# Moving mixer work between slots: frequencies, first convolution, ranks, and the second experts' preparation

## The chip, the cores and the metric

The kernel runs on one core of one Trainium2 chip. A core has five engines with queues of their own, each of which takes its instructions strictly in order: TensorE (PE in the profile; PEld are its weight loads), VectorE (DVE), ScalarE (ACT), GpSimd (POOL) and SyncE (SP), which here only issues DMAs. They wait for each other by semaphores. The metric is the device time of one execution in microseconds (us). Before the change, three runs gave 2046.63, 2048.35 and 2057.33 us; the median is 2048.35 us.

## The reference, cut to what matters

The whole is two macaron layers over 8 sequences of 256 tokens, 128 features each: a cell FFN, attention, the cell FFN again, then experts, a mixer, and the same experts a second time. The change lies in the last three:

```python
x = x + 0.5 * _L1_ffn_ref(_layernorm(x), gate_w, w1, w2, w3)      # first experts
x = x + _L1_attn_ref(_layernorm(x), ...)                          # the mixer
x = x + 0.5 * _L1_ffn_ref(_layernorm(x), gate_w, w1, w2, w3)      # second experts
```

The experts choose the two best of 8 gates for each token, scale the token by them, and apply two matmuls with a `silu` and a third. The mixer has a forward and a backward branch of this kind, and a Fourier branch:

```python
x = silu(_causal_dwconv(x, conv_w, conv_b))
x_dbl = einsum('bdl,ed->bel', x, xproj_w)
dt, Bm, Cm = (x_dbl[:, :r], x_dbl[:, r:r + n], x_dbl[:, r + n:])
delta = softplus(einsum('brl,dr->bdl', dt, dtproj_w) + dt_bias)
dA = exp(einsum('bdl,dn->lbdn', delta, -exp(A_log)))
dBu = einsum('bdl,bnl,bdl->lbdn', delta, Bm, x)
# scan over l: h = dA * h + dBu;  y = sum over n of h * Cm, + Dp * x, all times silu(z)
...
xc = silu(conv(fftn(x)) + fft_conv_b); x_out = ifftn(xc)
v = abs(x_out * max(silu(z))); out_f = (v - mean(v)) / sqrt(var(v) + 1e-05)
y = out + out_b[:, :, ::-1] + out_f;  return einsum('bdl,od->blo', y, out_proj_w)
```

## The kernel before

The tokens are cut into 4 chunks of 512 (two sequences each). All work of experts and mixer is placed by hand in numbered **slots** by `experts_and_mixer` (L799): `at(slot, f, ...)` files a function under a slot, and a loop at its end (L1582 to L1595) emits the slots one after the other, on TensorE, VectorE, ScalarE and GpSimd in just that order. Slot 32 c + s is called "slot s of chunk c" here; chunks are numbered 0 to 3. In each slot the loop emits a fixed core and then what was filed:

```python
scan(i)
feed(i + 1)
for f in before.get(i, ()):
    f()
if i % 2:
    sums(i - 3)
for f in after.get(i, ()):
    f()
...
spread(i + 2, *range(m, m + more))
```

The core handles one of 128 units (32 of each chunk). `spread` (L1179) puts delta times input (`pU`) and the delta (`p`) of the unit two slots ahead on all 128 partitions with 32-row matmuls, and ScalarE makes the decays `dA` of `p` (L1181). `feed` (L1188) multiplies `pU` by B on VectorE. `scan` (L1199) is the recurrence on VectorE; GpSimd multiplies its result by C (`hc`, L1201). `sums` (L1218) adds this up on TensorE every second slot. `pU` has two buffers, `h` two, `hc` four, and all other matmuls of the mixer share three PSUM banks (`bank`, L846). The number of decays made per slot, `more`, drops to 0 for two slots at each of two places of a chunk and catches up in the next five.

Between these stand, for the chunk that comes next (`ch`, filed from `o = (ch - 1) * UNITS`): `normalize` (L1027; layer norm, parts 0 and 1 are statistics, 2 and 3 the scaling on ScalarE), `features` (L1038; four transposes and a copy into `xT`), `convolve` (L1056; four matmuls each), `gate`, the `silu`s, `ranks` (L1087; two matmuls of 96 columns and the copy to `low`), `steps` (L1108; dt projection, ScalarE makes `ab` and `dl` of it), `softplus` (L1126) and `delta` (L1131; `dl` plus `ab` on VectorE, times `u` on GpSimd, then two DMAs on SP that make `du` with swapped halves). `steps`, `softplus` and `delta` run twice for each chunk, for two groups of channels `t`. For the Fourier branch, `frequencies` (L1230) is made of the next chunk's normalized tokens, `pairs` (L1241) on GpSimd, `mix` (L1251; ten matmul records and a copy) eight times, `mirror` (L1268) on GpSimd, then, from slot 27 into the next chunk, `halves` (`sp`, L1281), `over_channels` (L1297), `folds` (`t`, L1308), `over_tokens` (L1314), `squares` and the statistics, and at last `join` (L1396; GpSimd), `output` (L1402; sixteen matmul records) and `add` (L1418; GpSimd, the residual). In the last chunk the Fourier work is packed into the chunk itself. B and C rows are copied by DMA (`rows`, L1099) in slots 24, 26, 32 and 34.

The **second experts** (`class Experts`, L936) work on chunk c after its mixer residual is added. `prepare` (L1431) files `statistics` (VectorE and GpSimd) in slot k, `scale` (four activations that write `exn` on ScalarE) and `transpose` (four matmuls, copy to `exT`) in k + 1, `logits` in k + 2 and `gates` (VectorE) in k + 3. The buffer of `exn` is that of the mixer's `ab`, the one of `exT` that of `sz`. The matmuls of the experts themselves (`step`) follow from slot 129 on, one token tile to a slot, with the last two preparations among them: this is the tail.

Of the kernel before, what the change touches and what calls it, by code (L numbers as in the profile page):

```python
# [798 lines left out]
def experts_and_mixer(nc, tc, ident, nhalf, x, cols, ins, w, given, store):  # L799
# [19 lines left out]
    with ExitStack() as ctx:  # L819
# [23 lines left out]
        def at(slot, f, *a, last=False):  # L843
            (after if last else before).setdefault(slot, []).append(lambda: f(*a))
# [576 lines left out]
        def u_of(ch, t):  # L1421
            return lambda: (gots[ch]["u", t], None)

        def sz_of(ch):
            return lambda: (gots[ch]["sz"], None)

        def sc_of(ch, co):
            return lambda: (gots[ch]["sc"][:, co], fft_b[:, co : co + 1])

        first, second = Experts(given=given), Experts(store=store)  # L1430
        def prepare(experts, c, k, *room):  # L1431

            at(k, experts.statistics, c)
            at(k + 1, experts.scale, c, *room)
            at(k + 1, experts.transpose, c, last=True)
            at(k + 2, experts.logits, c, last=True)
            at(k + 3, experts.gates, c, last=True)
# [26 lines left out]
            return rooms["xn"][:, c % 2], rooms["xT"][:, c % 2]  # L1464

        end = NCH * UNITS
        prepare(second, 0, end - 9, room)
        prepare(second, 1, end - 4, room)
        for n in range(NCH * NT + 2):
            at(end + 1 + n, second.step, n)  # L1470
        prepare(second, 2, end + 3, room)
# [22 lines left out]
        for ch in range(NCH):  # L1494

            o = (ch - 1) * UNITS
            if ch == 0:
                at(-8, ranks, ch, 1)
                at(-8, largest, ch)
                at(-7, steps, ch, 0, 0)  # L1500
                at(-6, steps, ch, 0, 1)
                at(-6, exponentials)
                at(-6, softplus, ch)
            else:
                for part, k in enumerate((-23, -22, -1, -1)):
                    if ch == 1 and part < 2:
                        k = -6
                    at(o + (0 if ch == 1 and part > 1 else k), normalize, ch, part)
                at(o, features, ch, last=True)
                at(o + 2, convolve, ch, 1, 0)  # L1510
                at(o + 6, convolve, ch, 1, 1)
                at(o + 8, convolve, ch, 0, 0)
                at(o + 10, convolve, ch, 0, 1)
                at(o + 12, silu, u_of(ch, 1), u_of(ch, 0))
                at(o + 12, gate, ch, 0)
                at(o + 12, gate, ch, 1)
                at(o + 12, silu, sz_of(ch))
                at(o + 12, exponentials)
                at(o + 15, ranks, ch, 0)
                at(o + 16, ranks, ch, 1)  # L1520
                at(o + 17, steps, ch, 0, 0)
                at(o + 17, steps, ch, 0, 1)
                at(o + 18, softplus, ch)
                at(o + 22, largest, ch)
                at(o + 28, frequencies, ch, 0, last=True)
                at(o + 28, frequencies, ch, 1, last=True)
            at(o + (26 if ch == 0 else 19), delta, ch, 0, 0)
            at(o + (26 if ch == 0 else 19), delta, ch, 0, 1)
            v = o + (6 if ch == 0 else 0)
            at(v + 30, steps, ch, 1, 0)  # L1530
            at(v + 30, steps, ch, 1, 1)
            at(v + 31, softplus, ch)
            at(v + 32, delta, ch, 1, 0)
            at(v + 33, delta, ch, 1, 1)
            for r in range(2):
                at(o + 24 + 8 * r, rows, ch, r, 0)
                at(o + 26 + 8 * r, rows, ch, r, 1)
            o += UNITS
            for t in range(2):
                at(o + 16 * t + 3, skip, ch, t, 0)  # L1540
                at(o + 16 * t + 4, skip, ch, t, 1)
                at(o + 16 * t + 18, weigh, ch, t)
            if ch == 0:
                at(o - 2, frequencies, ch, 0)
                at(o - 1, frequencies, ch, 1, last=True)

            final = ch + 1 == NCH
            for k in (1, 2):
                at(o + (k - 1 if final else 2 * k + 4), pairs, ch, k)
            mixes = (6, 8, 10, 11, 13, 14, 16, 17) if final else (11, 13, 18, 20, 22, 23, 24, 25)  # L1550
            for k, v in enumerate(mixes):
                at(o + v, mix, ch, k // 2, k % 2, last=True)
                if k % 2:
                    at(o + v + 1 + (v == 13 and not final), mirror, ch, k // 2)
            k = o + (19 if final else 27)
            bursts.add(k)
            if not final:
                bursts.add(o + 12)
            at(k, silu, *(sc_of(ch, co) for co in range(4)))
            at(k, exponentials)  # L1560
            at(k + 2, halves, ch, 0)
            at(k + 3, halves, ch, 1)
            late = (8, 9, 10, 11) if final else (9, 10, 12, 14)
            for i in range(4):
                at(k + 4 + i, over_channels, ch, i // 2, i % 2, last=True)
                at(k + (6, 7, 8, 9)[i] + (not final), folds, ch, i // 2, i % 2)
                at(k + late[i], over_tokens, ch, i // 2, i % 2, last=True)
                at(k + late[i] + 1, squares, ch, i // 2, i % 2)
            rest = (13, 14, 15, 16, 17, 18, 18) if final else (16, 17, 18, 20, 22, 31, 32)
            at(k + rest[0], magnitude, ch)  # L1570
            at(k + rest[1], moments, ch, 0)
            at(k + rest[2], moments, ch, 1)
            at(k + rest[3], whiten, ch, 0)
            at(k + rest[3], whiten, ch, 1)
            at(k + rest[4], join, ch)
            at(k + rest[5], output, ch)
            at(k + rest[6], add, ch)
# [55 lines left out]
def tile_kernel(ctx: ExitStack, tc: tile.TileContext, ins, out):  # L1633
# [98 lines left out]
    with tc.tile_pool(name="w_mixer", bufs=1) as wp:  # L1732
        names = ("inT", "inK", "xproj", "dtT", "sel", "FT", "ysel", "outT", "G")
        w = load(wp, names, "s_")
        w["conv"] = wp.tile([P, 2, 5, 2 * DI], F32, name="w_conv")
        w["D"] = wp.tile([P, 4, P], F32, name="w_D")
        experts_and_mixer(nc, tc, ident, nhalf, x, cols, ins, w | w_moe, given, store)
# [124 lines left out]
```

## Time and profile before

| stretch | us |
|---|---|
| median of the runs | 2048.35 |
| the profiled execution | 2048.99 |
| its span, first to last instruction | 2047.2 |
| before slot 0 of the mixer (FFNs, attention, set-up) | 1425.1 |
| slots 0 to 127 of the mixer | 547.1 |
| tail: second experts | 75.0 |

| what | mean us of one | times, whole kernel |
|---|---|---|
| `scan` on VectorE, L1199 | 2.28 | 128 |
| `feed` on VectorE, L1188 | 1.22 | 128 |
| `hc` on GpSimd, L1201 | 2.36 | 128 |
| one `dA` activation on ScalarE, L1181 | 0.68 | 256 |

The span is counted from the first instruction to the last; the execution's own time is 1.8 us longer. Starts of slots are the starts of their scans. The stage table that follows in the prediction gives, for each stretch of the span, the time that each engine was busy and how many instructions it ran; then the granted TensorE clock as a share of full speed, the share of DMA time and the traffic. Rows in order of time give start, length, engine, line, operation, written and read tiles, and in brackets how long the engine sat idle before, and what ended that. Records of TensorE overlap, since matmuls are pipelined.

### The profile page before, as it was taken

What the parts mean: (1) busy time and instruction counts of PE and PEld (TensorE: products, weight loads), DVE (VectorE), ACT (ScalarE), POOL (GpSimd) and SP (SyncE); (2) the same over time, 40 slices, a digit from 0 to 9 for tenths busy, and PEclk for the clock granted to TensorE, in tenths of its full rate; (3) what the DMA queues carried; (4) which work ended last, traced back from release to release, by engine and by line L of the source; (5) the groups of instructions that cost most, each with busy time, mean ns of one, the idle gap of its engine ahead of it and who ended that gap; (6) DMA issues with size and microseconds to landing.
All of it is one profiled execution on the core that took longest, in us unless ns stands there. A gap on an engine that the chain in (4) does not pass through costs nothing. (4 is left out here: it accounts for less than half of the span.)

```text
span 2047.2 us, 45119 instructions
## 1 busy us (share of the span) xinstructions
PE 1936.4 (95%) x17792; PEld 1131.6 (55%) x17792; DVE 1559.3 (76%) x2669; ACT 1143.3 (56%) x2197; POOL 809.2 (40%) x919
## 2 busy tenths in 40 slices
PE   6999999997999999899999999889999999989888
PEld 4666666654565666566666665554343344344345
DVE  5777777776777777677777778555988897898874
ACT  3777777753333232377777776445546654654444
POOL 3000000115666665300000001444777878788763
PEclk9999999998999999999999999789999999999899
DMA  4000000000000000000000000202000000000000
GB/s 146 3 2 3 3 3 3 3 2 1 2 2 2 2 2 2 2 3 3 3 3 3 3 3 3 109 22 73 11 21 21 1 22 21 11 21 11 1 1 21
DMA packets 21239, 29.23 MB, mean 14 GB/s; under 512 B 12506, under 2 KB 13914, under 8 KB 20260
## 3 DMA queue, kind: packets, MB, share of 16 engines
q1 hardware_dynamic: 20740, 26.15, 4.3%
q8 instruction: 141, 2.31, 0.5%
q14 instruction: 70, 0.57, 0.1%
q10 hardware_dynamic: 288, 0.20, 0.0%
HBM read 16.10 MB, written 1.05 MB: 8 GB/s over the span
## 5 line engine op out<-in xcount | busy, mean ns | idle before, releaser
L344 DVE TENSOR_REDUCE negmax<-sc 128x2 f32<-128x512 f32 x768 | 490.7, 681 | 158.6 <-PE sc L338 158.2
L349 ACT ACTIVATE ex<-sc 128x512 f32<-128x512 f32 x768 | 420.9, 609 | 199.4 <-PE sc L338 199.1
L338 PE MATMUL sc<-qk,qk 32*128 32x256 f32 x6144 | 471.4, 405 | 10.7 <-DVE negmax L344 9.9
L338 PEld LDWEIGHTS sc<-qk,qk 32*128 32x128 f32 x6144 | 295.8, 186 | 147.4 <-ACT ex L349 100.8
L1201 POOL TENSOR_TENSOR hc<-h,C 128x1024 f32<-128x1024 f32 x128 | 301.4, 2356 | 112.2 <-DVE h L1199 108.0
L1199 DVE TENSOR_TENSOR_SCAN h<-dA,pU 128x1024 f32<-128x1024 f32 x128 | 292.1, 2282 | 12.8 <-DVE pU L1188 0.5
L299 ACT ACTIVATE qk<-pp,w_bqk,head_rows 128x256 f32<-128x256 f32 x384 | 197.3, 572 | 73.5 <-PE pp L419 34.7
L85 POOL TENSOR_SCALAR ln_ve<-ln_mv 128x2 f32<-128x2 f32 (+1 forms) x56 | 13.3, 237 | 550.5 <-DVE ln_mv L83 545.1
L1181 ACT ACTIVATE dA<-p,cols 128x512 f32<-128x512 f32 x256 | 162.2, 684 | 110.0 <-PE p L1179 108.0
L377 PE MATMUL pc<-ex,va 128*32 128x256 f32 x3072 | 206.0, 386 | 0.2 <-DVE y L442 0.2
L1188 DVE TENSOR_TENSOR pU<-pU,B 128x1024 f32<-128x1024 f32 x128 | 155.6, 1216 | 61.1 <-PE p L1179 52.1
L621 ACT ACTIVATE ex<-sc 128x512 f32<-128x512 f32 x128 | 66.1, 603 | 204.8 <-PE sc L606 204.8
L1179 PE MATMUL pU<-du,s_sel 32*128 32x512 f32 x512 | 147.5, 650 | 20.6 <-DVE h L1199 14.3
L1179 PE MATMUL p<-dl,s_sel 32*128 32x512 f32 x512 | 156.3, 643 | 4.3 <-ACT dA L1181 4.2
L606 PE MATMUL sc<-rot,rot 32*128 32x256 f32 x2048 | 135.2, 388 | 1.3 <-POOL rot L589 1.3
L377 PEld LDWEIGHTS pc<-ex,va 128*32 128x32 f32 x3072 | 80.7, 109 | 96.6 <-issue 61.8
L198 POOL TENSOR_SCALAR w_bqk<-pb,head_rows 128x2 f32<-128x2 f32 x12 | 3.5, 313 | 299.2 <-DVE pb L195 292.2
L606 PEld LDWEIGHTS sc<-rot,rot 32*128 32x128 f32 x2048 | 97.9, 184 | 36.2 <-issue 23.1
L624 POOL TENSOR_TENSOR both<-ex 128x512 f32<-128x512 f32 x64 | 80.0, 1272 | 71.2 <-ACT ex L621 71.2
L616 DVE TENSOR_REDUCE anegmax<-sc 128x2 f32<-128x512 f32 x128 | 79.4, 684 | 24.5 <-PE sc L606 24.5
L1179 PEld LDWEIGHTS pU<-du,s_sel 32*128 32x128 f32 x512 | 40.7, 186 | 91.2 <-issue 69.0
L988 DVE TENSOR_TENSOR hid<-ph,gate 128x1024 f32<-128x1024 f32 x32 | 39.1, 1221 | 66.1 <-PE ph L983 64.5
(292 smaller groups left out, 3173.1 us busy)
## 6 DMA issues: line engine op xcount, KB each, us to landing
qk<-turned SPq DMA_DIRECT2D x768, 1.0 KB
s_fft<-s_fft SPq DMA_DIRECT2D x5, 1024.0 KB
du<-ab SPq DMA_DIRECT2D x16, 256.0 KB
B<-low SPq DMA_DIRECT2D x64, 32.0 KB
C<-low SPq DMA_DIRECT2D x64, 32.0 KB
x<-x SPq DMA_DIRECT2D x4, 256.0 KB
s_inK<-s_inK SPq DMA_DIRECT2D x1, 1024.0 KB
out<-x SPq DMA_DIRECT2D x4, 256.0 KB
```

Of the source, the lines that this page charges most:

```text
L299: nc.scalar.activation(t[:, g, :], pp, AF.Identity, scale=w["mask"][:, g : g + 1], bias=w["bqk"][:, c, i, g : g + 1],)
L338: nc.tensor.matmul(sc[:, t, :], lhs[:, t * P : (t + 1) * P], rhs, start=True, stop=True)
L344: nc.vector.tensor_reduce(sh[:, :, 4 * g + j], sc, AX.X, ALU.max, negate=True)
L349: nc.scalar.activation(ex, sc, AF.Exp, scale=FD**-0.5)
L377: nc.tensor.matmul(st["pc"][32 * j : 32 * j + 32, g, :], st[2][:, kt, 2 * j + g, :], st["ex", g, j][:, kt, :], start=(kt == 0), stop=(kt = ...
L606: nc.tensor.matmul(sc[j][:, t, :], lhs[r, part, t * P : (t + 1) * P] if part < 2 else sel[r, :], rhs[r, part, :] if part < 2 else st["nm"] ...
L624: nc.gpsimd.tensor_tensor(both, ex[:, :, 0], ex[:, :, 1], ALU.add)
L1179: nc.tensor.matmul(dst, w["sel"][rs, i, :], src[rs, :], start=True, stop=True)
L1181: nc.scalar.activation(dA, pA, AF.Exp, scale=rate)
L1188: nc.vector.tensor_tensor(dB, dB, bcast(gots[ch]["B", r], 2), ALU.mult)
L1199: nc.vector.tensor_tensor_scan(hf, af, bf, 0.0, ALU.mult, ALU.add)
L1201: nc.gpsimd.tensor_tensor(hc, h, bcast(gots[ch]["C", r], 2), ALU.mult)
```

## The change

Only slot numbers change. For chunks 2 and 3, the scaling part of `normalize` moves from slot -1 to -4 (counted from the start of the chunk before the one that is prepared; for chunk 3, -3 is slot 61 of the whole count), `features` from 0 to -3 and the first `convolve` from 2 to -2. For chunks 1 to 3, `ranks` moves from slots 15 and 16 to 14 and 15, the first `steps` and `softplus` from 17 and 18 to 16 and 17, the first `delta` from 19 to 20, and both `frequencies` from 28 to 26. The second group's `steps`, `softplus` and `delta` move two slots later: from 30 and 31 to 32 and 33 (slots 0 and 1 of the chunk itself), and from 32 and 33 to 34 and 35. Of the Fourier branch's end, except in the last chunk, `join` moves from slot 17 to 16, `output` from 26 to 28 and `add` from 27 to 30. The second experts' preparations of chunks 0 and 1 move from slots 119 to 122 and 124 to 127 to slots 100 to 103 and 104 to 107, that is slots 4 to 11 of the last chunk.

```diff
         end = NCH * UNITS
-        prepare(second, 0, end - 9, room)
-        prepare(second, 1, end - 4, room)
+        prepare(second, 0, end - 28, room)
+        prepare(second, 1, end - 24, room)
...
-                for part, k in enumerate((-23, -22, -1, -1)):
-                    if ch == 1 and part < 2:
-                        k = -6
-                    at(o + (0 if ch == 1 and part > 1 else k), normalize, ch, part)
-                at(o, features, ch, last=True)
-                at(o + 2, convolve, ch, 1, 0)
+                early = (-23, -22, -4, -4, -3, -2) if ch > 1 else (-6, -6, 0, 0, 0, 2)
+                for part in range(4):
+                    at(o + early[part], normalize, ch, part)
+                at(o + early[4], features, ch, last=True)
+                at(o + early[5], convolve, ch, 1, 0)
...
-                at(o + 15, ranks, ch, 0)
-                at(o + 16, ranks, ch, 1)
-                at(o + 17, steps, ch, 0, 0)
-                at(o + 17, steps, ch, 0, 1)
-                at(o + 18, softplus, ch)
+                at(o + 14, ranks, ch, 0)
+                at(o + 15, ranks, ch, 1)
+                at(o + 16, steps, ch, 0, 0)
+                at(o + 16, steps, ch, 0, 1)
+                at(o + 17, softplus, ch)
                 at(o + 22, largest, ch)
-                at(o + 28, frequencies, ch, 0, last=True)
-                at(o + 28, frequencies, ch, 1, last=True)
-            at(o + (26 if ch == 0 else 19), delta, ch, 0, 0)
-            at(o + (26 if ch == 0 else 19), delta, ch, 0, 1)
-            v = o + (6 if ch == 0 else 0)
+                at(o + 26, frequencies, ch, 0, last=True)
+                at(o + 26, frequencies, ch, 1, last=True)
+            at(o + (26 if ch == 0 else 20), delta, ch, 0, 0)
+            at(o + (26 if ch == 0 else 20), delta, ch, 0, 1)
+            v = o + (6 if ch == 0 else 2)
             at(v + 30, steps, ch, 1, 0)
             at(v + 30, steps, ch, 1, 1)
             at(v + 31, softplus, ch)
...
-            rest = (13, 14, 15, 16, 17, 18, 18) if final else (16, 17, 18, 20, 22, 31, 32)
+            rest = (13, 14, 15, 16, 17, 18, 18) if final else (16, 17, 18, 20, 21, 33, 35)
```

## The prediction

> **What bounds the kernel now.** I read the stage table first (one row for each chunk of 32 slots and one for the tail), then VectorE's rows in order of time inside a slot, then TensorE's waits. The first view cuts the mixer at the starts of the scans of slots 0, 32, 64, 96 and at the end of the last scan.
>
> ```profile
> core 0: us, PE busy (x) PEld busy (x) DVE busy (x) ACT busy (x) POOL busy (x), PEclk, DMA share, GB/s
> 1425.10:1553.90 128.80, 120.08 (x539) 47.02 (x540) 119.34 (x81) 72.70 (x114) 95.19 (x67) 0.97 0.06 14
> 1553.90:1691.10 137.20, 129.66 (x618) 57.08 (x616) 119.05 (x87) 79.40 (x126) 110.98 (x86) 1.00 0.07 16
> 1691.10:1828.20 137.10, 129.67 (x618) 57.08 (x616) 117.92 (x79) 79.40 (x126) 108.29 (x78) 1.00 0.07 16
> 1828.20:1972.20 144.00, 129.44 (x627) 63.47 (x625) 121.18 (x113) 66.21 (x110) 116.97 (x88) 0.92 0.03 7
> 1972.20:2047.20 75.00, 60.80 (x304) 39.43 (x304) 36.38 (x115) 33.74 (x56) 32.44 (x35) 0.94 0.04 15
> ```
>
> VectorE's scan (2.29) and feed (1.21) of a slot start 3.54 us after those of the slot before when nothing is late. So 32 slots cost at least 113.3 us, and the four chunks lie 15.5, 23.9, 23.8 and 30.7 above that. This excess is all that the change can touch. Part of it is VectorE's own other work; the rest is VectorE waiting for TensorE, as here in slots 17 to 20 of the third chunk (bracket: idle before, and what ended it):
>
> ```profile
> 1770.29 1.23 DVE L1188 TENSOR_TENSOR pU<-pU,B 128x1024 f32<-128x1024 f32 x1 [0.37 <-PE p L1179]
> ...
> 1775.12 1.23 DVE L1188 TENSOR_TENSOR pU<-pU,B 128x1024 f32<-128x1024 f32 x1 [1.18 <-PE p L1179]
> 1776.26 0.68 DVE L1394 TENSOR_TENSOR sz<-py,sz 128x512 f32<-128x512 f32 x1
> ...
> 1779.51 1.23 DVE L1188 TENSOR_TENSOR pU<-pU,B 128x1024 f32<-128x1024 f32 x1 [0.38 <-PE p L1179]
> 1780.65 2.06 DVE L1135 TENSOR_TENSOR dl<-dl,ab 128x1024 f32<-128x1024 f32 x1
> ```
>
> By the table TensorE looks fuller than VectorE (129.67 of 137.10 against 117.92). If it were the bound, moving its work between slots would bring nothing. [...]
>
> **Part 1: ranks, steps and softplus one slot earlier, the delta one later (three chunks).** In slots 17 to 21 of the third chunk the waits are 0.37, 1.18, 0.38 and 0.51, and 0.37 more in slot 24: 2.8. They follow from `steps` (two matmuls, 1.98 of TensorE) standing in slot 17 ahead of sums (1.07) and spread (2.1), with a mixing (2.5) after that. One slot earlier, ranks and steps fall in slots 14 to 16; before, TensorE idled 1.53 in slot 14 before its spread. Slot 17 keeps only sums and spread, 3.2 of its 3.54. The `dl` addition (2.06) moves from slot 19 to 20, between the mixings of 18 and 20, and costs the same there. Late next is `steps` in slot 16: its input, the second `low` copy, stands on ScalarE behind four whitenings (2.07). I take 2.3 of the 2.8: **-6.9** over three chunks. The join's 2.35 on GpSimd, one slot earlier, has two slots of slack before the sums that could notice.
>
> **Part 2: chunk starts.** Slots 64 to 67 take 23.1 where 14.2 is the floor: TensorE runs from 1683 to 1714 with no gap over 0.8. The change takes four transposes (0.6) and a convolution (3.70) out of slots 64 to 66 into 61 and 62, but brings `steps` (1.98) from 62 to 64. The six slots 62 to 67 hold the same TensorE work less the transposes, which fit an idle 1.42 in slot 61. Against that, the residual `add` (1.27 on GpSimd) comes from slot 59 to 62, ahead of the second halving (`sp`, 2.4), and a product on TensorE already waits 0.77 for that. Walking both queues from 1683: +0.5 for chunk 1 to 2, and -0.1 for chunk 0 to 1, which has no residual add. Chunk 2 to 3 has no features or convolution to move out and only takes: `steps` 1.98, the add's 1.27, and the `dl` addition in slot 98, where it is less hidden. I get slot 100 at **+2.2**.
>
> On SP the `du` copies go out with the delta, now behind the row copies of slots 32 and 34; they landed 3.3 after their issue (the transfer traffic of 1844.2 to 1847.5) and are read 10 slots later: zero. `exn` takes over the `ab` buffer that they read, and comes later than that landing: zero, and at most 1 if the delta of slot 99 slips.
>
> The price of the `dl` addition is disputed:
>
> ```profile
> 1696.51 1.39 DVE L1135 TENSOR_TENSOR dl<-dl,ab 128x1024 f32<-128x1024 f32 x1
> ...
> 1833.69 3.47 DVE L1135 TENSOR_TENSOR dl<-dl,ab 128x1024 f32<-128x1024 f32 x1
> 1833.92 2.16 POOL L1249 TENSOR_TENSOR sd<-xe 128x540 f32<-128x540 f32 x2
> ```
>
> [...] The rows give it a size: 1.1 to 1.3, plus the time that GpSimd works beside it (0.3, 1.0 and 2.2 for 1.39, 2.06 and 3.47). [...]
>
> **Part 3: frequencies from slot 28 to 26, output from 26 to 28.** 2.14 against 2.05 of TensorE: zero. Chunk 0 has no output and only takes 2.14 in slot 26; its cover is the 0.98, 0.34 and 1.42 for which TensorE waits for the scan before the spreads of slots 27 to 29. Without that, 2 for this chunk.
>
> **Part 4: the second experts' first two preparations, from slots 119 to 127 to slots 100 to 107.** One costs VectorE 1.7 (statistics, 1925.19 to 1926.87), 0.4 (logits) and 2.94 (gates, 1947.66 to 1950.60), together 5.1; TensorE 1.5 (transposes) and 1.06 (logits); GpSimd 1.95; ScalarE 2.5. The new place, slots 100 to 107:
>
> ```profile
> 1849.40:1879.90 30.50, 29.84 (x170) 15.08 (x163) 27.72 (x16) 13.80 (x24) 28.30 (x20) 1.00 0.00 1
> ...
> 1921.90:1972.20 50.30, 45.94 (x209) 24.32 (x201) 35.95 (x56) 20.36 (x37) 34.81 (x26) 0.86 0.00 1
> ```
>
> In the first row VectorE's floor is 28.3 and its waits are 2.2; three engines are full. There is no room: 10.2 of VectorE work comes on top. The transposes wait for `exn` on ScalarE, this for `ln_shift` on GpSimd, which stands behind hc(100). From the start of scan(100): statistics end at 5.2, hc(100) at 7.3, ln 9.1, first `exn` 9.6, transposes 11.2, a product 13.1, spread(103) 14.2; VectorE wants that at 11.0, so it waits 3.2. The second preparation in the same way waits 1.05, and two mixings 0.55 and 0.6. Behind the waiting transposes stand a product and the spread on TensorE; behind the waiting `exn` stand the `exT` copy and the decays of four slots later on ScalarE, which nobody misses at 3.2. Total 28.3 + 10.2 + 5.4 = 43.9 (43.7 by the walk) against 30.5: **+13.2**; slot 108 then finds its mixing done and drops a wait of 0.9.
>
> The old place, the second row above, shows the same mechanism:
>
> ```profile
> 1932.30 1.23 DVE L1188 TENSOR_TENSOR pU<-pU,B 128x1024 f32<-128x1024 f32 x1 [3.25 <-PE p L1179]
> ...
> 1933.96 1.48 PE L964 MATMUL p<-ident,exn 128*128 128x128 f32 x4 [1.72 <-ACT exn L116]
> ...
> 1940.79 1.23 DVE L1188 TENSOR_TENSOR pU<-pU,B 128x1024 f32<-128x1024 f32 x1 [4.84 <-PE p L1179]
> ```
>
> Without the preparations TensorE loses 1.72 + 1.31 + 0.91 and 1.60 + 1.42 + 0.91 = 7.9 there. What is left (42.4) is above VectorE's floor (31.9), so all 7.9 come back. Walking it at full clock gives 9.3, but the granted clock was 0.86 and may dip elsewhere: **-8.5**. The tail behind it starts no sooner than this: its first `silu` waits on ScalarE for the magnitudes (squares on GpSimd until 1975.3, `silu` at 1978.9), so dropping the gates from its start is worth nothing more (up to 4 if that chain were short).
>
> **Sum**, against the profiled execution's 2048.99: -6.9 + 0.4 + 2.2 + 13.2 - 0.9 - 8.5 = -0.5. Each new wait also costs a hand-over of about 0.13 (the scan's idle after its feed), for some 12 waits 1.5: **2050.0**. The median of the runs, 2048.35, lies 0.6 below the profiled one.
>
> **Rivals.**
> - *GpSimd holds `ln_shift`* (slower). In slots 97 to 103 it runs without a gap and starts hc(100) 1.85 late; the change adds 1.95 per preparation, the late `ab` and the add. If it falls over 4 us behind, `exn` blocks ScalarE, the transposes block TensorE, and each preparation stalls VectorE by 8 rather than 3.2 and 1.05: about +11, 2061. Against: a dozen slots offer it 42 us of floor for about 52 of work, but VectorE's own stretching gives that time.
> - *The waits of part 1 only move*, to the mixings of slots 20 to 25 or behind the whitening: +6.9, 2057. For it: TensorE's row is nearly full.
> - *The end gives back more* (faster). If slots 119 to 127 fell to VectorE's floor, 18 would return instead of 8.5, and the tail began earlier: 2050 - 10 - 2, 2038. Against: TensorE's 42.4 there.
>
> **Chances.** Forecast 0.60 (2042 to 2057), GpSimd holds 0.17, waits move 0.13, end gives more 0.10. Range 2041 to 2061. A measurement here can tell about 0.5% (10 us) from no change: faster 0.09, same 0.73, slower 0.18.
>
> **What would show it.** Slots 81 to 85 in about 20 instead of 22.7; slots 100 to 107 in 42 to 46 with feed waits of 3 in slot 102 and 1 in slot 106; slots 119 to 127 in 41 to 43 with no wait above 2; slot 96 about 7 earlier. I am wrong if the waits of slot 18 persist, or if slots 100 to 107 take under 40 or over 48.

## The result: slower by 1.2 per cent

The changed kernel takes 2078.98 us in the median of four runs (2066.41 to 2079.09), the kernel before 2049.26 in the runs beside it (2046.63 to 2057.33). The ratio formed from all these runs (not from the medians, which lie 1.45% apart) is 1.0123, 95% interval 1.0076 to 1.0170; the ratios below are of the same kind. The profiled run took 2079.09, its span is 2077.3, 30.1 above the span before. The forecast was 2050.0.

**Profile after.** The same table by stage as before: the four chunks from scan to scan, then the tail (columns as in the first table of the prediction; the last but two is TensorE's granted clock, PEclk).

```profile
1427.90:1565.50 137.60, 128.84 (x536) 49.46 (x536) 119.15 (x81) 71.53 (x114) 96.97 (x68) 0.90 0.06 14
1565.50:1711.10 145.60, 140.17 (x618) 60.19 (x616) 119.75 (x86) 79.83 (x126) 111.28 (x86) 0.93 0.07 15
1711.10:1850.00 138.90, 130.99 (x606) 56.66 (x604) 118.16 (x78) 77.50 (x120) 104.76 (x76) 0.95 0.06 15
1850.00:2002.10 152.10, 136.29 (x643) 66.09 (x643) 120.70 (x130) 69.82 (x116) 117.84 (x89) 0.90 0.03 7
2002.10:2077.30 75.20, 60.37 (x303) 39.12 (x301) 32.71 (x98) 34.17 (x57) 32.87 (x36) 0.94 0.04 15
```

The chunks cost 8.8, 8.4, 1.8 and 8.1 more; VectorE's work (510.5 in the five rows, 513.9 before) has not grown. The column to look at is the clock: 0.90, 0.93, 0.95, 0.90 where it was 0.97, 1.00, 1.00, 0.92. Over the whole span the mean clock went from 0.976 to 0.962. The clock is recorded as either 1.0 or 0.5, so these means are 98 us at half clock before and 158 after: 60 us more, by my estimate worth up to 30 of TensorE's time. That is as much as the loss; whether it is the cause is for the experiments to show.

By place, from the starts of the scans (us):

| slots | before | after | difference | forecast |
|---|---|---|---|---|
| ahead of slot 0 (code unchanged) | 1425.1 | 1427.9 | +2.8 | 0 |
| 17 to 22, chunks 0, 1, 2 | 27.4 each | 35.2, 33.1, 28.1 | +14.2 | -6.9 |
| 28 to 35 and 60 to 67 | 37.4, 37.3 | 39.3, 40.9 | +5.5 | +0.4 |
| 36 to 43 and 68 to 75 | 33.1 each | 32.3 each | -1.5 | 0 |
| 96 to 99 | 21.3 | 24.6 | +3.3 | +2.2 |
| 100 to 108 | 35.9 | 49.8 | +13.9 | +12.3 |
| 119 to 126 | 48.0 | 38.9 | -9.1 | -8.5 |
| slots 9 and 90, rest | | | +1.0 | +1.5 |

Part 4 went nearly as forecast in both places. The error is part 1. The next view of the changed kernel has slots 17 to 21 of the three chunks in rows 1 to 3, then slots 100 to 107 and 119 to 126.

```profile
1493.70:1523.60 29.90, 29.13 (x104) 11.12 (x102) 19.05 (x13) 13.14 (x21) 14.22 (x11) 0.71 0.00 1
1641.50:1669.20 27.70, 26.94 (x103) 10.85 (x101) 19.02 (x12) 12.79 (x20) 16.47 (x12) 0.75 0.00 1
1787.10:1809.90 22.80, 22.04 (x103) 8.60 (x101) 18.82 (x13) 12.68 (x20) 16.53 (x12) 0.93 0.00 1
1874.60:1920.00 45.40, 38.77 (x194) 21.26 (x188) 34.35 (x73) 20.61 (x37) 33.68 (x32) 0.89 0.05 12
1961.00:2002.10 41.10, 40.33 (x186) 20.52 (x179) 30.25 (x17) 15.14 (x25) 31.01 (x18) 0.89 0.00 1
```

The first three rows hold nearly the same instructions, and differ by 7.1 in time and by 0.71 to 0.93 in the clock. The kernel before has full clock there; its slots 17 to 21 of the first chunk:

```profile
1491.70:1514.40 22.70, 22.31 (x106) 9.01 (x104) 19.87 (x13) 13.13 (x21) 15.17 (x11) 1.00 0.10 24
```

VectorE's view of the third chunk of the changed kernel (slots 81 to 84; bracket: idle before) shows what part 1 does where the clock holds, which here is up to slot 83:

```profile
1790.08 1.23 DVE L1188 TENSOR_TENSOR pU<-pU,B 128x1024 f32<-128x1024 f32 x1 [0.67 <-PE p L1179]
...
1793.65 1.21 DVE L1188 TENSOR_TENSOR pU<-pU,B 128x1024 f32<-128x1024 f32 x1
...
1797.55 1.21 DVE L1188 TENSOR_TENSOR pU<-pU,B 128x1024 f32<-128x1024 f32 x1
...
1804.07 1.23 DVE L1188 TENSOR_TENSOR pU<-pU,B 128x1024 f32<-128x1024 f32 x1 [2.89 <-PE p L1179]
1805.21 1.22 DVE L1135 TENSOR_TENSOR dl<-dl,ab 128x1024 f32<-128x1024 f32 x1
```

The waits of slots 18 and 19 are gone, as forecast. But one of 2.89 stands in slot 20, part of it at half clock (1799.3 to 1802.7), and slot 17 waits 0.67 where it waited 0.37. In the first chunk three more stand in slots 17 to 19 (the feeds at 1498.77, 1504.37 and 1511.12 waited 2.77, 1.95 and 2.74). TensorE's view and the clock of that place:

```profile
1493.26 1.98 PE L1115 MATMUL p<-low,s_dtT 64*128 64x512 f32 x4
1495.17 1.84 PE L1179 MATMUL pU<-du,s_sel 32*128 32x512 f32 x4
1496.78 1.93 PE L1179 MATMUL p<-dl,s_sel 32*128 32x512 f32 x4
```
```profile
1492.10:1495.50 3.40, 3.40 (x9) 1.27 (x10) 3.27 (x3) 2.93 (x6) 3.14 (x3) 1.00 0.00 0
1495.50:1509.20 13.70, 13.70 (x36) 5.49 (x34) 8.03 (x6) 5.93 (x10) 5.36 (x3) 0.50 0.00 0
```

The spreads take 1.84 and 1.93 instead of 1.13 and 1.03. Half clock starts at 1495.5 and lasts 13.7, four times 3.41 (each of the 40 stretches of half clock that end inside the two traces lasts one to five times 3.41), although TensorE was busy for 3.40 of the 3.40 before it. So idle time does not explain it. What is small in that stretch is the part of the array in use: "64*128" and "32*128" in the rows are the rows and columns of a matmul's weights. Four half-height steps and four quarter-height spreads, at 0.43 each (a pair takes 1.13, one alone 0.70), make 4 x 0.43 x 0.5 + 4 x 0.43 x 0.25 = 1.3 of 3.41, 0.38 of the array.

I reckoned this share (time x rows x columns, per 3.41 us, from all TensorE rows of both traces, with 0.43 for 512 columns from each matmul's start; an estimate, since the ends of matmuls are modelled). Of 40 onsets of half clock in these two traces, 37 follow a stretch of at most 0.39; of 40 returns, 39 follow one of at least 0.72. Four stretches of at most 0.39 had no onset and three of 0.76 to 0.82 no return (the first 38 us, which have no clock record, left out). By rows alone about 30 of the 40 onsets follow at most 0.39. TensorE's busy share ahead of these onsets runs from 0.02 to 1.00; it is above 0.9 only twice, both times at the start of slot 17 of the changed kernel, with the steps of part 1 over 64 rows.

In the changed kernel the stretch just ahead of the half clock of slots 17 to 19 has a share of 0.36 in chunk 0 and of 0.34 in chunk 1. In chunk 2, where the pieces of 3.41 us lie otherwise against the program, the one at the start of slot 17 has 0.41, and the clock holds. **Theory C** (clock), a guess for the runs to test, is then: the small share of that stretch brings the half clock of slots 17 to 19, so part 1 alone has it too, and with more rows in use it goes. Rival **Q**: the new order of TensorE's queue is worse by itself.

### The profile page after: what moved, and what is told of

Read it like the earlier page. It is cut to its first block, busy times and chain, and to the rows that moved or that the text cites. A ratio compares the mean times of both kernels' runs of the same rounds, so it can differ in the third digit from the quotient of the medians.

```text
span 2077.3 us, 45122 instructions
## 1 busy us (share of the span) xinstructions
PE 1965.5 (95%) x17792; PEld 1140.5 (55%) x17792; DVE 1556.1 (75%) x2669; ACT 1145.7 (55%) x2197; POOL 809.9 (39%) x919
## 3 DMA queue, kind: packets, MB, share of 16 engines
HBM read 16.10 MB, written 1.05 MB: 8 GB/s over the span
## 5 line engine op out<-in xcount | busy, mean ns | idle before, releaser
L1179 PE MATMUL pU<-du,s_sel 32*128 32x512 f32 x512 | 155.3, 680 | 17.2 <-DVE h L1199 12.8
L1179 PE MATMUL p<-dl,s_sel 32*128 32x512 f32 x512 | 162.6, 676 | 5.0 <-ACT dA L1181 5.0
```

Source lines behind the costliest of these rows:

```text
L1179: nc.tensor.matmul(dst, w["sel"][rs, i, :], src[rs, :], start=True, stop=True)
```

## The experiments

Sixteen kernels, times against runs of the kernel before on the same chip (medians there 2048.5 to 2051.0).

**Part 1 alone, and the rows in use.** e1 is the kernel before with part 1. e2 to e4 widen the low-rank matmuls: nothing is added or moved, but the ranks give 128 columns and the steps read 128 rows. The added weight rows of the steps are zero.

```diff
-            px = bank([P, CT])[0:LOW, :]
+            px = bank([P, CT])
+                k = (2 * r + t) * LOW
...
-                    px, w["xproj"][:, r, t, :], got["u", t][:, r, :], start=(t == 0), stop=(t == 1)
+                    px, w["xproj"][:, k : k + P], got["u", t][:, r, :], start=(t == 0), stop=(t == 1)
...
-                got["low"][0:DR, r, :],
+                got["low"][:, r, :],
```

> The kernel before with part 1 alone: ranks, steps, softplus of chunks 1 to 3 one slot earlier, the first delta one slot later. [...] Theory Q (queue): the new order makes VectorE wait for TensorE whatever the clock; the same slots are long, also where the clock is 1.0; about 2056. The prediction's own theory: 2042 (6.9 less), no wait in slots 17 and 18.

Measured 2068.05, ratio 1.0089 (1.0074 to 1.0105): part 1, forecast at -6.9, costs 18. In its profile slots 17 to 21 take 31.5 in chunk 0 (clock 0.67), 22.8 in chunks 1 and 2. Where the clock was whole in slots 17 and 18, slot 18 took 3.92 against 5.20 before and slot 17 4.3 against 4.0; so Q is wrong there. Of the 20.3 by which its span is longer, 10.9 lie in slots 17 to 22 of the three chunks; 6.3 lie in slots 60 to 67, where nothing was moved and 17 us of half clock fell.

> The changed kernel with the ranks written for 128 columns instead of 96 and the steps reading 128 rows instead of 64 (the added weight rows are zero, the result is the same). No instruction is added or moved, and the time of a matmul at full clock does not depend on its rows. Theory C: the stretch before slot 17 rises from 0.36 to about 0.6 of the array, the half clock in slots 17 to 20 of chunks 0 and 1 goes, these slots take about 17 to 20 each instead of 26 and 24, and the kernel is about 12 to 16 faster than the changed kernel: 2063 to 2067. Theory Q: the rows in use change nothing, 2079.

Measured 2063.0, ratio to before 1.0068 (1.0052 to 1.0084): 16 less than the changed kernel in the medians, as C said (by the ratios 0.55%; their intervals just overlap). The same three rows of TensorE in the first chunk:

```profile
1493.69 1.98 PE L1116 MATMUL p<-low,s_dtT 128*128 128x512 f32 x4
1495.60 1.13 PE L1180 MATMUL pU<-du,s_sel 32*128 32x512 f32 x4
1496.56 1.03 PE L1180 MATMUL p<-dl,s_sel 32*128 32x512 f32 x4
```

The steps take 1.98 over 128 rows as over 64, and the spreads behind them run at full speed. The clock of slots 17 to 21 is 1.00 in chunk 0 (22.4 us instead of 29.9) and 0.93 in chunks 1 and 2.

> The kernel before with the same widening: control. It has no half clock in slots 14 to 24, so both theories expect the same time, 2049 within 3.

Measured 2050.45, ratio 0.9999 (0.9986 to 1.0013). The widening itself costs and brings nothing.

> The kernel before with part 1 and the widening. Theory C: with the clock kept, part 1 brings what the prediction gave it, some 2 to 3 per chunk: 2038 to 2045, and no half clock in slots 16 to 19. Theory Q: as with part 1 alone, about 2056.

Measured 2059.65, ratio 1.0051 (1.0035 to 1.0068). (Its profiled run was its fastest, 2052.70.) C missed: 8 came back of 18, but no gain appeared. The half clock of slots 17 to 19 is gone (3.9 and 3.5 in slots 18 and 19 of all chunks), yet slot 20 takes 5.8 at full clock, and 7.4 or 9.0 with a half clock that comes there. VectorE in slots 19 and 20 of chunk 1, e4 and then e8, which leaves the first delta in slot 19:

```profile
1645.19 1.23 DVE L1189 TENSOR_TENSOR pU<-pU,B 128x1024 f32<-128x1024 f32 x1 [1.26 <-PE p L1180]
1646.33 1.22 DVE L1136 TENSOR_TENSOR dl<-dl,ab 128x1024 f32<-128x1024 f32 x1
```
```profile
1642.86 1.21 DVE L1189 TENSOR_TENSOR pU<-pU,B 128x1024 f32<-128x1024 f32 x1
1643.97 2.54 DVE L1136 TENSOR_TENSOR dl<-dl,ab 128x1024 f32<-128x1024 f32 x1
...
1649.33 1.23 DVE L1189 TENSOR_TENSOR pU<-pU,B 128x1024 f32<-128x1024 f32 x1 [0.62 <-PE p L1180]
```

TensorE's skip (the `Dp` term, 1.13) and sums (1.07) stand ahead of the spread there. In slot 19 the addition gave TensorE 2 us to get through them; moved to slot 20 it comes after the wait, and VectorE pays for both. It also shifts GpSimd's products, and a VectorE instruction of slot 22 on 128x4 elements takes 0.90 instead of 0.25 beside one of them. That is **theory D**; the runs that follow bear out its times, but not all of its mechanism.

**The delta's place.**

```diff
-            at(o + (26 if ch == 0 else 20), delta, ch, 0, 0)
-            at(o + (26 if ch == 0 else 20), delta, ch, 0, 1)
+            at(o + (26 if ch == 0 else 19), delta, ch, 0, 0)
+            at(o + (26 if ch == 0 else 19), delta, ch, 0, 1)
```

> Part 1 and the widening, but with the first delta left in slot 19. In e4 slots 17 and 18 lost their wait, but slot 20 rose from 3.5 to 5.8 at full clock (the seeds and sums that stand before its spread on TensorE, which the delta's addition of 2.05 had covered while it stood in slot 19), and slot 22 rose by 0.65 (a small VectorE instruction beside a GpSimd one). Theory D (the delta's move uncovers these): slot 19 about 5.6, slot 20 3.5 to 4, slot 22 4.7; 1 to 2 less per chunk than e4, and less half clock in slot 20 as the stretch ahead is stretched or filled differently (uncertain). Rival: the addition only adds to slot 19 and slot 20 stays at 5.8 or more, then it is slower than e4 by 2 per chunk.

Measured 2050.99, ratio 1.0001 (0.9987 to 1.0015), 0.5% under e4, the time that D expected. Slot 19 takes 5.8, slot 20 4.3, slot 22 4.7, with some half clock left in slots 19 and 20.

> The widened changed kernel with the first delta back in slot 19. Theory D (the delta's move uncovers TensorE's delay in slot 20 and, with the light stretch ahead of it, calls the half clock there): as between e4 and e8, 3 per chunk less, 2051 to 2058. Rival (the delta's place does not matter, the rest of the change is what is left): 2063.

Measured 2057.55, ratio 1.0038 (1.0022 to 1.0054), 5.5 under e2: D's time again, inside the whole change. Its slots 17 to 21 run at clock 1.0 in all chunks. They take 21.16 and 21.15 in chunks 1 and 2 instead of 22.69, and slot 22 5.04 instead of 4.74; in chunk 0 22.34 instead of 22.68, since the steps come late there (slot 17: 5.6). So with the clock whole and the delta in its place, the gain is 1.2, 1.2 and nothing, 2.4 for the 6.9 forecast.

D's mechanism does not hold at full clock. Slots 19 and 20 of chunk 1 together, in e4 (delta in slot 20) and in e11 (delta in slot 19):

```profile
1638.10:1647.50 9.40, 8.64 (x40) 3.68 (x40) 8.01 (x7) 4.18 (x7) 5.84 (x3) 1.00 0.00 1
```
```profile
1638.40:1647.70 9.30, 8.54 (x40) 3.58 (x40) 9.17 (x7) 4.18 (x7) 6.53 (x8) 1.00 0.00 1
```
```profile
1641.69 2.55 DVE L1136 TENSOR_TENSOR dl<-dl,ab 128x1024 f32<-128x1024 f32 x1
```

From scan to scan it is 9.35 against 9.31. In slot 19 the addition takes 2.55 (the last row, of e11), with 1.46 of a GpSimd product beside it, and nothing waits; in slot 20 it takes 1.22, and VectorE waits 1.26. So at full clock the delta's place costs only in slot 22, 5.39 against 5.04, 0.4 a chunk. The rest comes with half clock: one stretch of it makes the two slots 10.9 to 11.0 long with the delta in slot 20 and 10.0 to 10.1 with it in slot 19. Over all profiles with part 1 it began there in 13 of 18 chunks with the delta in slot 20 and in 7 of 15 with it in slot 19, too few to tell. Why the medians differ by 5 to 9 (e2 to e11, e4 to e8) is thus only in part explained.

> Part 1 with the first delta left in slot 19, not widened: the missing corner beside e1 (18 slower: narrow, delta in 20), e4 (10 slower: wide, delta in 20) and e8 (0: wide, delta in 19). If the clock at slots 17 to 19 and the delta's place cost separately, this is some 8 to 9 slower than before, 2056 to 2060, with the long half clock from slot 17 in chunks 0 or 1. If the light stretch needs both, it is 2049 to 2052.

Measured 2065.29 (2052.11 to 2079.62), ratio 1.0062 (1.0040 to 1.0084). That is slower than the 2056 to 2060 expected if the costs are separate. The long half clock is there, this time in chunk 2 (slots 81 to 85 in 30.9), and not in chunks 0 and 1. The corners are thus narrow 1.0089 and 1.0062, wide 1.0051 and 1.0001 (delta in slot 20, in slot 19). The narrow steps cost 0.4 to 0.6% in either place, clear of the intervals. The delta's place costs 0.3 to 0.5%; that is clear for the wide steps, while for the narrow ones the intervals overlap. In the profiles, half clock begins in slot 17 in 4 of the 9 chunks of the three kernels with narrow steps (the changed kernel, e1, e15), and in slots 17 and 18 in none of the 24 of the eight kernels with part 1 and wide ones.

**The other parts alone.** e5 moves only the two calls of `prepare` for the second experts; e6 has only parts 2 and 3; e7 is e2 with the preparations back at the end.

> The kernel before with part 4 alone: the second experts' first two preparations in slots 100 to 107 instead of 119 to 127. The prediction's sum: slots 100 to 107 43.7 to 45.4 instead of 30.5, slot 108 0.9 to 1.0 less, slots 119 to 127 8.5 to 9.1 less: 3.8 to 4.8 slower in all, 2054 against 2050. Theory C (clock) expects the same slots and, in both places, half clock where transposes and the tiny gate matmuls leave the array idle: net half-clock time about as before, 2052 to 2058. Rival G (GpSimd holds ln_shift) expects 8 per preparation, 2061 or more.

Measured 2051.38, ratio 1.0017 (1.0004 to 1.0030), 2.8 to 3.5 slower. Slots 100 to 107 take 41.9, slot 108 gives 1.0, slots 119 to 126 take 39.9. The rival on GpSimd is out.

> The kernel before with parts 2 and 3 alone: features, convolution and normalization before the chunk ends, frequencies in slot 26, output and residual add later, the second group's steps, softplus and delta two slots later. The prediction's sum: 2.6 slower, 2053. Theory C: as slots 28, 29 (chunk 0) and 60, 61 lose TensorE work, a stretch of about 0.35 of the array appears before slots 29 to 31, 62 to 63 and 94 to 95, where the changed kernel lost 1.8, 3.4 and some of its 3.3; so 2055 to 2060, with half clock in these places and nothing lost in slots 17 to 22. Rival Q (the order itself, full clock): the loss is in slots 32 to 36 and 96 to 99, with the clock at 1.0.

Measured 2050.65, ratio 0.9995 (0.9978 to 1.0011): no change; both theories expected a loss. In its profile C's half clock is there, in slots 29 and 30 (slot 31: 5.3 instead of 3.5) and from slot 94 to 96 (slots 96 to 99: 4.1 more), though not in slots 60 to 63; one of 3.4 in slots 19 and 20 costs 1.6. Against that, slots 32 to 43 and 64 to 75 gain 1.0 and 0.9, slots 100 to 107 1.2, slots 119 to 126 1.5 and the tail 1.2.

> The changed kernel with the second experts' preparations back in slots 119 to 127, and with the widened ranks and steps. If the parts add up, this is e2 less what part 4 costs (4 to 5): about 2058. If part 4 pays for itself at the end (the rival that the end gives back more), it is 2063 or slower.

Measured 2052.76, ratio 1.0013 (1.0001 to 1.0025), 10 under e2 and not 5. Why taking part 4 out of the whole change brings more than e5 shows was not settled.

The parts of the change alone, 1.0089, 1.0017 and 0.9995, add up to 1.0101; the whole is 1.0123 with an interval of 1.0076 to 1.0170.

**More work against half clock.** If theory C holds in the idle stretches too, spare matmuls there should make the kernel faster.

```diff
+        def spare():
+            nc.tensor.matmul(bank([P, CT]), ident, w["inT"], start=True, stop=True)
+
+        for slot in (115, 116, 117, 118):
+            at(slot, spare)
```

These are the slots of e13; e9, e10 and e12 use those that they name.

> The kernel before plus eleven spare matmuls (128 x 128 weights, 512 columns, some 0.9 of TensorE each; nothing reads their results) in slots where TensorE waits: 8, 25, 46, 57, 78, 89, 115 to 118, 125. Nothing else is changed, so only work is added. Theory C (clock): each lifts its stretch by about 0.25 of the array; the half clock of slot 8, of slots 26 and 90 (1.7 each when it comes), and of slots 117 to 121 goes; 4 to 8 faster, 2041 to 2046, and a mean clock above 0.98. Rival: the clock follows something else than the array's use; then the spare work changes nothing or costs up to 0.9 each, 2049 to 2055.

Measured 2066.02, ratio 1.0077 (1.0057 to 1.0097): C's forecast failed as a whole. In slots 25, 57 and 89 the spare matmul took a PSUM bank that ScalarE's copy had to free, waited 2.80 for it, and so ran after the idle stretch and ahead of the mixing: slots 26, 58 and 90 take 8.1 to 8.5, half clock included. In slots 115 to 118, where a bank was free, there was no half clock until slot 121, and slots 119 to 126 took 45.4 instead of 48.0.

> The widened changed kernel plus eighteen spare matmuls in its idle slots (8, 25, 28 twice, 57, 60 twice, 89, 92 twice, 101, 102 twice, 105, 106, 116 to 118). Theory C: the half clock at slots 8, 26, 29 to 31, 58, 62, 90, 94 to 96, 102, 105 and 117 to 120 goes: 6 to 12 faster than e2, 2051 to 2057. Rival: no change against 2063, or slower by up to 0.9 per spare matmul on the path (2063 to 2072).

Measured 2066.04, ratio 1.0070 (1.0045 to 1.0096): no gain on e2, for the same reason (slots 26 and 58: 8.5 and 9.6; slot 102: 10.6 instead of 8.6).

> Candidate: e8 (ranks and steps one slot earlier and widened, delta in its old slot) with the spare matmuls of e9. Theory C: e8 (equal to the kernel before) less what e9 gains: 2041 to 2046. Rival: as e8, 2050, or slower.

Measured 2057.67, ratio 1.0036 (1.0023 to 1.0050): the spare work of e9 costs here too (slots 58 and 90: 8.5 and 8.1).

> The kernel before plus one spare matmul (128 rows, 128 columns of weights, 512 columns; about 0.9 of TensorE, read by nothing) in each of slots 115 to 118, where TensorE waits 1.3 per slot for VectorE. In e9 the half clock of slots 117 to 120 was gone with them, and slots 119 to 126 took 45.4 instead of 48.0 to 49.3. Theory C: the same here, no half clock between slots 115 and 120, slots 119 to 126 45 to 46, time 2 to 4 less: 2045 to 2047. Rival: no change.

Measured 2048.59, ratio 0.9984 (0.9971 to 0.9998): only the four spares at the end, 2.4 to 3.3 faster. Among sixteen kernels, one interval that misses 1 by so little may be chance.

> The same spare matmuls in the same slots, but over 32 rows: as long on TensorE, with a quarter of the array in use. Theory C (time x rows x columns): each adds only 0.06 to its stretch, so the half clock of slots 117 to 120 stays, and slots 119 to 126 take 47.4 to 49.4. Rival B (the clock follows the time in which TensorE is busy, whatever the rows): the half clock goes as in e13, and slots 119 to 126 take 45 to 46.

Measured 2051.29, ratio 1.0005 (0.9987 to 1.0023). The stretch by stretch rows of both (1917.5 to 1924.3), e13 first:

```profile
1917.50:1920.90 3.40, 3.04 (x19) 0.77 (x18) 3.27 (x3) 0.18 (x1) 2.21 (x2) 1.00 0.00 0
1920.90:1924.30 3.40, 2.15 (x11) 0.70 (x11) 3.27 (x3) 1.18 (x3) 3.40 (x3) 1.00 0.00 0
```
```profile
1917.50:1920.90 3.40, 1.99 (x14) 0.71 (x10) 3.27 (x3) 0.51 (x1) 2.22 (x2) 1.00 0.00 0
1920.90:1924.30 3.40, 1.97 (x9) 0.85 (x9) 3.27 (x3) 0.76 (x2) 3.40 (x3) 0.51 0.00 0
```

With 128 rows the clock holds until 1925.9, in slot 119, and then falls for 3.4, where the kernel before had 13.7 from slot 117 on; with 32 rows it falls at 1921.0 for 10.2, and slots 119 to 126 take 54.7 in this profile against 45.9. This agrees with C, but is one profile of each: the same slots took 54.8 in e15, which has no spares, and 53.0 in e16, which has those of e13. Nor does it by itself refute the busy-time rival (B): the 32-row spare of slot 117 ran beside a spread (0.69 beside 0.70, from 1915.7), so TensorE was busy for only 1.99 where it was 3.04. What refutes it is the changed kernel against e2: 3.40 busy of 3.40, the same instructions, half clock behind the 64 rows and none behind the 128, as in the other kernels with part 1 (4 of 9 chunks against none of 24).

**A kernel without the faults.**

> Candidate: parts 1 to 3 widened, the first delta in slot 19, the second experts' preparations in their old slots, and the spare matmuls of e13. Theory C and D together: e7 (4 slower than before) less 5.5 (e2 to e11), less 3 (e13): 2044 to 2048. Rival (the losses do not add): 2050 to 2056.

Measured 2051.14, ratio 0.9992 (0.9976 to 1.0008). The sum expected from C and D, 2044 to 2048, missed: the losses are gone, and with them nothing is won. In its profile slots 17 to 22 gain 1.2 each in chunks 1 and 2, but slots 119 to 126 take 53.0 instead of 48.0, with half clock from 1923.1 for 6.8 and from 1933.3 for 17.1. So the four spares do not keep the clock in every run. No version here beats the kernel before by more than e13's 0.16%.

## Why the prediction was wrong

- **What bounds the kernel.** Right in kind: VectorE waits for TensorE. Not seen: that the durations of TensorE are not fixed (four matmuls of a spread took 1.03 at full clock and 1.93 at half). All of them were taken at full clock, and the clock column, 0.97 to 1.00 in chunks 0 to 2, was taken as given. The one place with 0.86 was discounted as "may dip elsewhere".
- **Part 1, first failed step:** "Slot 17 keeps only sums and spread, 3.2 of its 3.54." The step priced the new order in time alone; part 1 alone cost 18 (e1) where -6.9 was forecast. It put 1.98 of half-height steps straight against quarter-height spreads; behind that stretch, with its share of 0.36, the clock was 0.50 for 13.7, and slots 17 to 19 became 6 each. Widening the rows alone takes 0.4 to 0.6% off (e1 to e4, e15 to e8, changed kernel to e2).
- **Part 1, second failed step:** "I take 2.3 of the 2.8", which is too much also at full clock. Slot 18 falls to 3.9 and slot 19 to 3.5 as forecast, but slot 17 takes 4.4, in chunk 0 5.6, for 4.0 before. "The `dl` addition (2.06) moves from slot 19 to 20 [...] and costs the same there" is right for the sum of the two slots (9.35 against 9.31) but not as it was meant: the addition falls to 1.22, and a wait of 1.26 comes to slot 20. Slot 22, which the sum did not have, takes 0.65 more. Slots 17 to 22 thus gain 0.9 in chunk 1 (e4) and lose 0.3 in chunk 0 (e2) where the clock is whole. Leaving the delta in slot 19 takes 0.3 to 0.5% off; how, is shown in part only.
- **Part 2.** At chunk 2 to 3, forecast +2.2, measured +3.3 with 10.2 of half clock ahead of it. At the other two starts forecast +0.4, measured +5.5; 5.1 of that is slots 31 and 63, behind half clock that follows stretches with shares of 0.25 in slot 28 and 0.36 in slot 61. The frequencies had left slots 28 and 60; in e10, with two spare matmuls in each of these, there was no half clock from slot 28 to 34 and from 60 to 67. Alone (e6) these parts cost nothing. The walks behind these sums took the `dl` addition in its new slots at 1.3 to 1.6, the author's estimate, which no run shows there: in the changed kernel it took 2.16, 2.16 and 1.88 in slots 34, 66 and 98.
- **Part 3.** "Zero" holds in slot 26 (6.46 both times in chunk 0, 4.77 and 4.78 in chunk 1).
- **Part 4.** The times are right: +14.9, -1.0, -9.1 for +13.2, -0.9, -8.5. In the new place the mechanism is the one forecast, with the wait of slot 102 at 4.71 instead of 3.2 and that of slot 106 at 3.87 instead of 1.05:

```profile
1890.00 1.23 DVE L1188 TENSOR_TENSOR pU<-pU,B 128x1024 f32<-128x1024 f32 x1 [4.71 <-PE p L1179]
```

  TensorE idled 4.22 for `exn`, and its next 3.4 ran at half clock. In e5, where the clock was whole in slot 102, the wait is 2.72, and the part alone costs 11.4 there. In the old place the sign "no wait above 2" failed: slot 120 waits 5.41, with 17.1 of half clock from slot 116 on (20.5 in three stretches before). That the sum fits so well is partly luck.
- **Rivals.** "The waits of part 1 only move", 2057, was the nearest: a wait did come to slot 20, and a smaller one stayed in slot 17. At full clock that leaves part 1 little gain; the loss itself, the clock, no case had. GpSimd did not hold `ln_shift`. The range ended at 2061, since no term of the sum could change the speed of an engine.

## What to carry to other kernels

Before moving TensorE work, look at the clock of each stretch and at the rows and columns of what will stand side by side; here, half clock of 13.7 us stood behind matmuls over 64 and 32 rows next to each other, and widening some of them with zero rows was free (1.98 both times; e3 at 0.9999) and left slots 17 to 21 of that chunk at 1.00 (e2). Before moving an elementwise instruction out of a slot, ask who uses the time that it takes: in slot 19 the addition was the cover of TensorE's delay, and what it saved by moving (2.55 to 1.22) came back as a wait of 1.26. A saving of 2 us in one slot is worth testing only together with the clock, since one half-clock stretch of 3.41 us cost up to 1.6 in slots 19 and 20.

## What was not expected of the hardware

- Half clock came in multiples of 3.41 us (one to five, 40 times in the two traces), and TensorE's busy time alone does not tell where: busy 3.40 of 3.40, at a share of 0.36 by my estimate, was followed by 13.7 at half clock. There it lasted through shares of 0.49, 0.68 and 0.65 and ended behind one of 0.95.
- Where the stretches lie against the program differs from run to run: part 1 lost its time in chunk 0 in e1, in chunk 2 in e15, in chunks 0 and 1 in the changed kernel. Part of the scatter of the runs (e15: 2052 to 2080, with mean clocks of 0.974 to 0.960) goes with this.
- Dead work may have made a kernel faster (e13), by 0.16% (interval 0.02 to 0.29%); with it in e16 nothing was gained.
- The same addition on VectorE took 1.22 in one slot and 2.55 in another, with 0.12 and 1.46 of a GpSimd product beside it: the prediction's price for it (1.1 to 1.3 plus the time beside) holds in e4 and e11.
- A VectorE instruction on 128x4 elements took 0.90 instead of 0.25 beside a GpSimd product, and ended within 0.03 of it.
